# Column sums of two softmaxes taken in quarters on quarters of the array, and their inverses spread through DRAM

## The chip, the core and the metric

The kernel runs on one core of a Trainium2 chip. The metric is device time in microseconds (us) of one execution, lower is better. Five engines work side by side, each through its own queue: TensorE (PE in the profile, with its weight loads as PEld), VectorE (DVE), ScalarE (ACT), GpSimd (POOL) and SyncE (SP), which here only issues DMA transfers.

## What is computed

Four layers follow one another on `x`, eight samples of 512 channels by 1024 positions, float32. Layers 1 and 2 are the ones that matter here: each is an attention over the 1024 positions with a softmax, and the softmax needs one sum of exponentials for every position.

```python
# layer 1 (x: 8 samples, 512 channels, N = 1024 positions)
h = _group_norm(x, gamma, beta).reshape(B, C, N)
q, k, v = wq @ h + bq, wk @ h + bk, wv @ h + bv          # written as einsums
logits = jnp.einsum('bcn,bcm->bnm', q, k) * scale
attn = jax.nn.softmax(logits, axis=-1)                   # e / sum over m of e
o = jnp.einsum('bnm,bcm->bcn', attn, v)
x = x + wp @ o + bp
...
# layer 2 (t, p, g of 128 channels each)
s = jnp.einsum('ncq,nck->nqk', t, p)
s = jax.nn.softmax(s * SCALE, axis=2)                    # e / sum over k of e
att = jnp.einsum('nqv,ncv->ncq', s, g)
z = Z_w @ att                                            # then an affine map, and + x
```

Layer 0 is an attention without a softmax, divided by the largest singular value of its map; layer 3 multiplies signs of the activations by signs of weights and applies a piecewise linear function.

## The kernel before

A first stage of some 230 us loads all inputs, makes layer 0's maps and folds layer 1's four weight matrices into two. Then the function `fast` runs once for each of the eight samples, in some 210 us each: layer 1, layer 2 and layer 3 of that sample, with the beginning of the next sample's work woven in. Everything is float32 on TensorE but for layer 3's signs. Products of layer 1 are done with seven block products in place of eight (`seven`, `product_of`, `values1`).

The exponentials are kept transposed: a tile `e` holds 128 of the summed-over positions on its partitions and all 1024 output positions along its rows. A softmax's denominator is therefore a sum over partitions and over eight tiles `e`. VectorE adds the eight tiles into one tile `esum` of 128 x 1024, and TensorE adds over the partitions, with a matrix of ones as weights. That last step, the inverse, and the spreading of the inverse over all 128 partitions is the function `inverse_sums` (lines 822 to 844), which the change rewrites. Before the change it does this:

- Two matmuls (line 826), one for each half of the positions (`half(h)`, 512 columns). The weights are 64 columns of ones, so each matmul writes 64 equal rows: half 0 to partitions 0 to 63 of one PSUM bank (`side(0)`), half 1 to partitions 64 to 127. A float32 matmul is two instructions in the trace, so these are four.
- One VectorE reciprocal of the whole bank, 128 x 512 (line 834), into the tile `rsum`.
- Four DMAs (line 838), each of 64 partitions by 2 KB: each half of `rsum` is copied to both halves of the partitions of `rfull`, which is 128 x 2 x 512. After that each partition holds all 1024 inverses.
- Two DMAs of 2 KB (line 840) that copy the inverses to four rows of `guard`, a table that is checked once at the end of the kernel (`count_bad`); if a value in it is out of bounds, a slower general version is run.

`inverse_sums` is called at two places, 15 times in all. For layer 1 it is called in all eight samples, in the middle of the product `make_v` (line 916); the inverse is first used in `values1` (line 593), after the rest of `make_v` and the first eight groups of `values1`' products. For layer 2 it is called in the first seven samples (line 969); the eighth uses `inverse_rows`, which has no DMA on its path and is not changed.

The layer 2 call is the tight one. TensorE's order around it is written out in `fast`, and the trace has it in that order: two eighths of the product for half 0 (`values2(0, range(0, 2))`), then `inverse_sums`, then the other six eighths for half 0 and four eighths for half 1 (lines 970 to 972, matmuls at line 951), and then `close2` (line 674), which multiplies by `att`. `att` is that product times the inverses (line 960, on VectorE). So the inverse must go through the reciprocal, the DMA and the `att` multiply in the time of 10 products, or TensorE waits. After `close2` the rest of the sample follows, in `leave` (layer 3) and in `make_u` of the next sample.

Within an engine's queue instructions start in order, and waits are on semaphores. All DMAs named here are issued by SyncE, which has the loads of `x`, the stores of the output and the stores and loads of `f_dram` in the same queue. `f_dram` is a scratch array in DRAM: layer 0's map `f` is written to it (line 1365) and read back per sample (line 282).

Of the kernel before, what the change touches and what calls it, by code (L numbers as in the profile page):

```python
# [8 lines left out]
F32 = mybir.dt.float32  # L9
# [7 lines left out]
P = 128  # L17
B = 8
C = 512
N = 1024  # L20
CC = C // P
NT = N // P
HF = 512
NH = N // HF
NTH = HF // P
MID = 64
# [59 lines left out]
def kernel(  # L86
# [17 lines left out]
    nc = tc.nc  # L104
# [9 lines left out]
    dram = ctx.enter_context(tc.tile_pool(name="dram", bufs=1, space=bass.MemoryType.DRAM))  # L114
# [8 lines left out]
    def bank():  # L123
        return psum["bank"].tile([P, HF], F32, tag="bank", name="bank")
# [17 lines left out]
    def half(i):  # L142
        return bass.ts(i, HF)

    def side(i):

        return slice(i * MID, (i + 1) * MID)
# [93 lines left out]

    f_dram = [dram.tile([P, HF], F32, name=f"f_dram{b}") for b in range(B)]
    gm = [keep.tile([P, 3, P], F32, tag=f"gm{j}", name=f"gm{j}") for j in range(NPAIR)]
    sw3 = wpool.tile([P, CC, C // 2], F16, tag="sw3", name="sw3")
# [574 lines left out]

    def inverse_sums(env, esum, row):

        ps = bank()
        for h in range(NH):
            mm(  # L826
                out=ps[side(h), :],
                lhsT=ones2[:, 0:MID],
                rhs=esum[:, half(h)],
                start=True,  # L830
                stop=True,
            )
        r = env["small"].tile([P, HF], F32, tag="rsum", name="rsum", bufs=1)
        nc.vector.reciprocal(r, ps)  # L834
        full = env["small"].tile([P, NH, HF], F32, tag="rfull", name="rfull", bufs=1)
        for h in range(NH):
            for i in range(2):
                nc.sync.dma_start(out=full[side(i), h, :], in_=r[side(h), :])
        for h in range(NH):
            nc.sync.dma_start(  # L840
                out=guard[4 * row : 4 * row + 4, h, :],
                in_=r[h * MID : h * MID + 1, :].rearrange("o (a b) -> o a b", b=P),
            )
        return full

    def inverse_rows(env, esum, row):
# [31 lines left out]
    def fast(env, n, hb, ua):  # L878
# [35 lines left out]
        for k, _ in enumerate(make_v(hb, vt)):  # L914
            if k == 3:
                r = inverse_sums(env, esum, n)
            if k == 5:
                next(ahead, None)
            chore(2)
# [47 lines left out]
        values2(0, range(0, 2))  # L967
        if more:
            r = inverse_sums(env, esum, B + n)
            values2(0, range(2, NTH))  # L970
            att = values2(0, range(NTH, NT))
# [151 lines left out]
    env = {}  # L1123
# [252 lines left out]
    ps = bank()  # L1376
# [5 lines left out]
    ps = bank()  # L1382
# [83 lines left out]
    ones2 = late.tile([P, P], F32, tag="ones2", name="ones2")  # L1466
    nc.vector.memset(ones2, 1.0)
    guard = late.tile([2 * B * 4, NH, P], F32, tag="guard", name="guard")
# [3 lines left out]
    with ExitStack() as main:  # L1472
# [3 lines left out]
        small = main.enter_context(tc.tile_pool(name="small", bufs=3))  # L1476
# [122 lines left out]
    with tc.If(verdict[0] > 0):  # L1599
        with (  # L1600
# [5 lines left out]
            env = {"big": big, "e": epool, "small": small}  # L1606
# [49 lines left out]
```

## Time and profile before

| | us |
|---|---|
| median of three runs | 1911.45 (1911.01 to 1911.63) |
| the profiled execution, its own time | 1911.79 |
| its span, from the first instruction to the last | 1909.9 |
| TensorE busy in that span | 1886.4 |
| VectorE busy | 1130.2 |
| ScalarE busy | 510.3 |
| GpSimd busy | 224.5 |
| the 15 reciprocals of line 834 | 50.4 |

The profile shows one execution. A row of the timeline gives the start of a group of instructions, the time from the first one's start to the last one's end, the engine, the line, the operation with output and inputs, the shape, and how many; in brackets stands how long the engine was idle just before and what ended that. Matmuls are pipelined: one of 512 columns in float32 is listed with 592 ns, but in a row of them each starts about 0.43 us after the one before, so their listed lengths overlap.

### The profile page before, as it was taken

To read this page: it belongs to the slowest core of one execution; us is meant where nothing else is said; L and a number is where in the kernel's file an instruction comes from. 1 tells how busy PE (TensorE), PEld (TensorE's weight loads), DVE (VectorE), ACT (ScalarE), POOL (GpSimd) and SP (SyncE) were. 2 spreads that over 40 slices of the span, in tenths; PEclk is the share of its full clock that TensorE was granted. 3 is DMA by queue.
4 is the path that set the end of the run, shared out by engine and by line. 5 is a ranking of instruction groups with operands and counts; after the bars stand their busy time and mean duration, and the time that the engine had idled before them with its cause. 6 is when DMAs were issued, how large, how long until landed. Compare 5 with 4: busy or idle time off the path is not lost.

```text
span 1909.9 us, 16334 instructions
## 1 busy us (share of the span) xinstructions
PE 1886.4 (99%) x6118; PEld 977.5 (51%) x6118; DVE 1130.2 (59%) x1762; ACT 510.3 (27%) x811; POOL 224.5 (12%) x176
## 2 busy tenths in 40 slices
PE   9999999999999999999999999999999999999997
PEld 4366456544745447444645446544645455544653
DVE  3256676448664677447664676457753775466547
ACT  2142121134212332035202431034202521234014
POOL 0000011201121011200121011201120011101121
PEclk9999999999999999999999999999999999999999
DMA  8420000002000120002000120002000200010001
GB/s 320 159 78 6 0 6 12 1 12 88 17 1 0 34 72 12 1 11 88 17 1 0 38 68 12 0 13 87 11 1 9 91 12 0 1 34 22 12 0 46
DMA packets 27782, 66.45 MB, mean 35 GB/s; under 512 B 4272, under 2 KB 5424, under 8 KB 27056
## 3 DMA queue, kind: packets, MB, share of 16 engines
q1 hardware_dynamic: 26768, 64.90, 10.1%
q8 instruction: 50, 0.82, 0.2%
q10 hardware_dynamic: 864, 0.43, 0.1%
q14 instruction: 36, 0.29, 0.1%
q0 software_dynamic: 64, 0.00, 0.0%
HBM read 38.51 MB, written 18.87 MB: 30 GB/s over the span
## 4 chain that ended last, share of the span: by engine, by line
PE 92%; DVE 7%; issue 1%; ACT 1%; DMA 0%; POOL 0%; DVEq 0%; ACTq 0%
PE bank L387 42%; PE bank L556 20%; PE bank L951 6%; PE bank L805 6%; PE bank L1241 5%; PE bank L657 3%; PE bank L411 2%; PE bank L674 2%; DVE both L748 1%; DVE both L718 1%; PE wide L1281 1%; PE wide L1335 1%; PE bank L1022 1%; PE bank L1023 1%; PE bank L697 1%; PE bank L826 1%
## 5 line engine op out<-in xcount | busy, mean ns | idle before, releaser
L556 PE MATMUL bank<-e,vt 128*128 128x512 f32 x768 | 334.2, 593 | 0.0
L556 PEld LDWEIGHTS bank<-e,vt 128*128 128x128 f32 x768 | 144.9, 190 | 174.8 <-issue 173.2
L387 PE MATMUL bank<-ut,h 128*128 128x512 f32 x384 | 182.3, 597 | 0.0
L344 DVE TENSOR_TENSOR e<-bank,e 128x512 f32<-128x512 f32 x128 | 87.8, 686 | 81.9 <-PE bank L387 80.8
L387 PE MATMUL bank<-us,hs 128*128 128x512 f32 x256 | 121.5, 597 | 1.3 <-DVE us L316 0.5
L387 PEld LDWEIGHTS bank<-ut,h 128*128 128x128 f32 x384 | 71.4, 190 | 95.6 <-issue 84.0
L951 PE MATMUL bank<-e,tpg 128*128 128x512 f32 x256 | 114.7, 595 | 0.0
L805 PE MATMUL bank<-tpg 128*128 128x512 f32 x256 | 114.6, 592 | 0.0
L812 ACT ACTIVATE e<-bank 128x512 f32<-128x512 f32 x128 | 76.4, 597 | 128.6 <-PE bank L805 128.6
L387 PE MATMUL bank<-h,wu 128*128 128x512 f32 x192 | 90.4, 593 | 2.4 <-DVE h L462 1.7
L387 PE MATMUL bank<-wo,h 128*128 128x256 f32 x384 | 91.8, 382 | 0.0
L817 DVE TENSOR_TENSOR esum<-esum,e 128x1024 f32<-128x1024 f32 x48 | 58.8, 1225 | 54.9 <-ACT e L812 54.9
L359 POOL TENSOR_TENSOR e<-e 128x512 f32<-128x512 f32 x32 | 43.4, 1356 | 403.8 <-ACT e L338 238.3
L951 PEld LDWEIGHTS bank<-e,tpg 128*128 128x128 f32 x256 | 48.1, 190 | 63.2 <-issue 63.1
L805 PEld LDWEIGHTS bank<-tpg 128*128 128x128 f32 x256 | 48.6, 190 | 60.7 <-issue 60.5
L387 PEld LDWEIGHTS bank<-wo,h 128*128 128x128 f32 x384 | 71.6, 190 | 13.5 <-ACT vt L338 4.1
L359 POOL TENSOR_TENSOR ut<-ut 128x512 f32<-128x512 f32 x16 | 21.7, 1359 | 476.1 <-ACT ut L340 476.1
L344 DVE TENSOR_TENSOR vt<-bank,vt 128x512 f32<-128x512 f32 x64 | 44.1, 689 | 56.2 <-PE bank L387 55.8
L387 PEld LDWEIGHTS bank<-us,hs 128*128 128x128 f32 x256 | 47.1, 190 | 54.9 <-issue 48.3
L834 DVE RECIPROCAL rsum<-bank 128x512 f32<-128x512 f32 x15 | 50.4, 3358 | 38.2 <-PE bank L826 38.2
L685 ACT ACTIVATE sg<-xt,rb 128x512 f16<-128x512 f32 x64 | 45.0, 718 | 103.7 <-DVE xt L676 100.2
L1241 PE MATMUL bank<-xt,fg 128*64 128x512 f32 x256 | 59.5, 613 | 4.6 <-DMA fg<-in_w_fg 4.6
(330 smaller groups left out, 3017.2 us busy)
## 6 DMA issues: line engine op xcount, KB each, us to landing
xt<-in_x SPq DMA_DIRECT2D x55, 512.0 KB
out<-both SPq DMA_DIRECT2D x63, 256.0 KB
rfull<-rsum SPq DMA_DIRECT2D x60, 128.0 KB
f_dram<-f SPq DMA_DIRECT2D x8, 256.0 KB
fb<-f_dram SPq DMA_DIRECT2D x8, 256.0 KB
w<-in_w SPq DMA_DIRECT2D x1, 1024.0 KB
q<-in_w_q SPq DMA_DIRECT2D x1, 1024.0 KB
k<-in_w_k SPq DMA_DIRECT2D x1, 1024.0 KB
```

What stands on the lines that cost most here:

```text
L344: nc.vector.tensor_tensor(dst, ps, u, ALU.add)
L359: nc.gpsimd.tensor_tensor(c22, c22, c12, ALU.add)
L387: mm(out=ps[:, q * w : (q + 1) * w], lhsT=lt(ka, kb, q, k), rhs=rhs(ka, kb, q, k), start=first and q == 0 and k == 0, stop=last and k == 1 ...
L556: mm(out=ps, lhsT=a[:, t, bass.ts(r_, P)], rhs=e[t], start=first and t == 0, stop=last and t == NTH - 1, skip_group_check=True,)
L657: mm(out=ps[:, i, :], lhsT=xt[:, cc, bass.ts(4 * h + i, P)], rhs=sbw["tpg"][:, cc, 2 * P : 3 * P], start=cc == 0, stop=cc == CC - 1,)
L685: nc.scalar.activation(sg[:, cc, :], xt[:, cc, half(h)], AF.Sign, bias=rb3[:, cc : cc + 1])
L805: mm(out=ps, lhsT=pt[:, 0, bass.ts(t, P)], rhs=tt[:, 0, half(h)], start=True, stop=True,)
L812: nc.scalar.activation(e[:, half(h)], ps, AF.Exp, scale=float(P) ** -0.5)
L817: nc.vector.tensor_tensor(esum, esum, e, ALU.add)
L834: nc.vector.reciprocal(r, ps)
L951: mm(out=banks[h], lhsT=gt[:, t, :], rhs=es[t][:, half(h)], start=t == 0, stop=t == NT - 1,)
L1241: mm(out=banks[i][side(h), :], lhsT=w0[i][:, cc, :], rhs=xt[:, cc, half(h)], start=cc == 0, stop=cc == CC - 1,)
```

## The change

`inverse_sums` works on quarters of the positions. Four matmuls take the place of two: each has 32 columns of ones as weights and 256 positions, and writes 32 equal rows to its own quarter of the partitions, at its own quarter of the array's columns (`tile_position`). The reciprocal is then of 128 x 256. One row of each quarter (partitions 0, 32, 64 and 96, 1 KB each) is written by one DMA to a new scratch array in DRAM, `r_dram[row]`, of 4 KB; one DMA reads these 4 KB 128 times, once for each partition of `rfull` (512 KB in all), and one more reads them into the four rows of `guard`. There are 16 arrays `r_dram`, one for each row number, so none is used twice. Both reads need the write to have landed, and all three are issued by SyncE.

```diff
+    r_dram = [dram.tile([4, N // 4], F32, name=f"r_dram{i}") for i in range(2 * B)]
     f_dram = [dram.tile([P, HF], F32, name=f"f_dram{b}") for b in range(B)]
...
     def inverse_sums(env, esum, row):
 
+
+        g, w = 4, N // 4
         ps = bank()
-        for h in range(NH):
+        for q in range(g):
             mm(
-                out=ps[side(h), :],
-                lhsT=ones2[:, 0:MID],
-                rhs=esum[:, half(h)],
+                out=ps[bass.ts(q, P // g), 0:w],
+                lhsT=ones2[:, 0 : P // g],
+                rhs=esum[:, bass.ts(q, w)],
                 start=True,
                 stop=True,
+                tile_position=(0, q * P // g),
             )
-        r = env["small"].tile([P, HF], F32, tag="rsum", name="rsum", bufs=1)
-        nc.vector.reciprocal(r, ps)
+        r = env["small"].tile([P, w], F32, tag="rsum", name="rsum", bufs=1)
+        nc.vector.reciprocal(r, ps[:, 0:w])
+        nc.sync.dma_start(
+            out=r_dram[row], in_=r.rearrange("(q i) n -> q i n", q=g)[:, 0, :]
+        )
         full = env["small"].tile([P, NH, HF], F32, tag="rfull", name="rfull", bufs=1)
-        for h in range(NH):
-            for i in range(2):
-                nc.sync.dma_start(out=full[side(i), h, :], in_=r[side(h), :])
-        for h in range(NH):
-            nc.sync.dma_start(
-                out=guard[4 * row : 4 * row + 4, h, :],
-                in_=r[h * MID : h * MID + 1, :].rearrange("o (a b) -> o a b", b=P),
-            )
+        nc.sync.dma_start(
+            out=full.rearrange("p h n -> p (h n)"),
+            in_=r_dram[row].rearrange("q n -> (q n)").partition_broadcast(P),
+        )
+        nc.sync.dma_start(
+            out=guard[4 * row : 4 * row + 4, :, :],
+            in_=r_dram[row].rearrange("(h j) (a b) -> (j a) h b", h=NH, b=P),
+        )
         return full
```

## The prediction

> **What bounds the kernel now.** I read the shares of the page first, then a table of stages, then the timeline around one call of the changed function.
>
> ```profile
> PE 1886.4 (99%) x6118; PEld 977.5 (51%) x6118; DVE 1130.2 (59%) x1762; ACT 510.3 (27%) x811; POOL 224.5 (12%) x176
> ```
>
> Busy shares of engines in three stretches (us, then busy and count for PE, PEld, DVE, ACT, POOL, then clock, DMA share, GB/s):
>
> ```profile
> 230.00:1890.00 1660.00, 1659.19 (x5044) 857.30 (x5043) 1009.32 (x1469) 445.73 (x701) 205.50 (x142) 1.00 0.07 23
> 1890.00:1910.00 20.00, 9.77 (x36) 3.79 (x34) 13.47 (x21) 10.04 (x16) 7.87 (x6) 0.85 0.30 109
> 0.00:230.00 230.00, 217.40 (x1042) 116.39 (x1043) 107.44 (x273) 54.54 (x96) 11.11 (x28) 1.00 0.32 117
> ```
>
> From 230 to 1890 us, which holds all 15 calls, TensorE is idle for 0.8 us in 1660. Two rules follow there: TensorE time that is taken away shortens the run, and any wait that the change puts on TensorE lengthens it. VectorE time is worth something only through a wait of TensorE.
>
> Timeline of TensorE at the first call for layer 2:
>
> ```profile
> 402.32 1.88 PE L951 MATMUL bank<-e,tpg 128*128 128x512 f32 x4
> 404.13 1.08 PE L826 MATMUL bank<-esum,ones 128*64 128x512 f32 x4
> 405.14 8.85 PE L951 MATMUL bank<-e,tpg 128*128 128x512 f32 x20
> 413.83 3.60 PE L674 MATMUL bank<-att,z 128*128 128x512 f32 x8
> ```
>
> The same call on VectorE and on SyncE's DMA queue:
>
> ```profile
> 405.26 3.36 DVE L834 RECIPROCAL rsum<-bank 128x512 f32<-128x512 f32 x1 [3.65 <-PE bank L826]
> 408.64 2.44 SPq L838 DMA_DIRECT2D rfull<-rsum  x4
> 411.13 1.30 SPq L840 DMA_DIRECT2D guard<-rsum  x2
> 411.70 0.69 DVE L960 TENSOR_TENSOR att<-bank,rfull 128x512 f32<-128x512 f32 x1 [3.09 <-DMA rfull<-rsum]
> ```
>
> The reader is to see two things. First, the four matmul instructions of line 826 take 1.08 us, not four times 0.43: the two halves of the array's columns run at the same time, so there are two rounds. Second, `att` ends at 411.70 + 0.69 = 412.39, and its user, line 674, starts at 413.83 directly behind the matmuls before it: 1.4 us to spare (1.0 us if its first weight load, at 413.40, is what must wait). The other six calls for layer 2 look the same within 0.1 us where I looked at them (626, 844, 1060 and 1681 us). For layer 1 the inverse is made at 287 us and first used at 315.8 us (line 593).
>
> **What the Trainium skill says.** "TensorEngine Tiling (Array Packing)", Available Configurations and Key Properties: with all 128 rows in use the array can be split in two tiles of 64 columns or four of 32; tiles run at the same time; a change of the mode drains the engine. The trace agrees for two tiles (the rounds above) and shows the drain; no run here shows four. "TensorE: Matmul & The Clock Gate", Measured speedup vs the span model: three column tiles of 32 gave 2.38 times, by a model of one matmul plus about 4 ns for each further tile. "DMA: Bandwidth & Descriptors", Rules for kernel authors: a DMA that reads what another wrote must wait for the first one's completion semaphore. The trace agrees: the first read of `f_dram` waited 1.4 us for its write. The same page, How many engines: a transfer over 4 partitions is spread over 4 of the 16 DMA engines. No run here shows that, and for 4 KB it is small.
>
> **The matmuls.** What a call costs TensorE now: the L951 row of four starts at 402.32, so in an unbroken row the next instruction would start at 402.32 + 4 x 0.428 = 404.03. (0.428 comes from the row of eight of line 674: 3.60 = 7 steps + 0.592.) The next L951 row starts at 405.14 and is 8.85 long where 19 x 0.428 + 0.592 = 8.72 would do. A call thus takes 405.14 - 404.03 + 0.13 = 1.24 us: two rounds of 0.428, and 0.38 around them for the changes of mode. After the change there are eight instructions of 256 columns. The 128x256 matmuls of line 387 in `make_v` step by (1.89 - 0.38) / 7 = 0.216 us. If four run at once, that is two rounds of 0.216, and with some 0.02 us for starting four one after another and the same 0.38 around them, 0.83 us. Gain 0.41 us per call, times 15 = 6.1 us. Bounds: 0 if only two of the four run at once (four rounds of 0.216), less than 0 only if they ran one by one, which the two-tile rounds speak against; at the top 0.45 us if the drain of a shorter matmul is shorter too, 6.8 us. I take 0.41. Weight loads double to eight; the four now are done within 0.20 us beside the matmuls, so I cost them at nothing.
>
> **The reciprocal.** 3.36 us for 512 columns, 0.16 us for the reciprocals of one column (line 1077), so for 256 about 0.16 + 3.20 / 2 = 1.76 us. VectorE gets 15 x 1.6 = 24 us back. Nothing waits for it but the inverse itself: for layer 2 VectorE is idle for 3.09 us just after it, and for layer 1 the use is 28 us away. Worth nothing on the path, except as time for the transfers.
>
> **The transfers.** They gain a wait: the read waits on SyncE for the write to land. Behind it in that queue stand only the guard's read and then, at 430 us, the stores of the output, so the queue itself blocks nobody. Worked out for the call at 404 us, with times of the trace before:
>
> - last matmul ends 0.41 us earlier, at 404.80; reciprocal from 404.85 to 406.61.
> - The write, 4 KB, issued at 406.63. Nearest row, `f_dram`:
>
> ```profile
> 106.48 1.02 SPq L1365 DMA_DIRECT2D f_dram<-f  x2
> 108.95 0.32 SPq L282 DMA_DIRECT2D fb<-f_dram  x1
> ```
>
> The read went out 2.47 us after the write's issue, for 256 KB and with another load under way: the upper bound. In the row of rfull above, the first bytes moved 1.1 us after the issue, by the DMA view, and `att` began about 0.5 us after the bytes of its half had moved: 1.6 us is the lower bound. I take 1.8: the read goes out at 408.45.
> - The read, 512 KB: 1.0 us to the first byte as above, 1.5 us at the 350 GB/s that loads of `x` reach, 0.5 us to land: 3.0 us, so 411.45. At the 200 GB/s at which the four copies move now it is 2.6 us of bytes, and 412.55.
> - `att` takes 0.69 us: done at 412.15. It is wanted at 413.83 - 0.41 = 413.42, or at 412.99 by the weight load.
>
> That leaves 0.8 to 1.3 us. The transfer chain is one link longer, and the halved reciprocal and the single issue in place of four (2.44 us of issuing) pay for it. With both upper bounds (write + 0.7, read + 1.1) `att` ends at 413.95 and TensorE waits 0.5 to 1.0 us, seven times: 3.7 to 6.7 us. For layer 1 any of this is hidden by 28 us of matmuls. The guard's read is wanted at the end of the kernel and costs nothing.
>
> **Sum.** 1911.79 of the profiled execution, less 6.1, is 1905.7; it stands 0.34 above the median, so 1905.35 against the median of 1911.45. A measurement of this kernel tells 0.2%, 3.8 us, from no change.
>
> **Rivals.**
>
> - *The broadcast is slow, and TensorE waits for it* (the slower side). One mechanism: 16 DMA engines read the same 4 KB of DRAM at the same time, and `att` waits for the whole 512 KB, where now it waits for the half that it uses. It decides from 411.45 + 0.85 on, that is, once the read takes over 3.9 us; it undoes the whole gain at 0.87 us more, and the run is slower by 0.2% from 1.4 us more. At 130 GB/s the bytes take 4.0 us, 2.5 more than taken; 1.65 us of wait, times 7, is 11.5 us: 1911.45 - 6.1 + 11.5 = 1916.9. For it: nothing in the trace reads the same few KB 128 times undisturbed. Against it: `bg_row`, 128 reads of the same 512 bytes, passes in the first 50 us without a gap in the DMA view. Chance 0.13.
> - *Four tiles run no better than two.* The time on TensorE is unchanged: 1911.4. For it: only two at once are seen here. Chance 0.13.
> - *A part of the gain is lost in short waits* (write and read near their upper bounds, half of the seven margins used up, 2.5 to 5 us): 1909. Chance 0.10.
> - *The order of instructions shifts.* Another length of the transfers could make the framework put some matmuls in another order, in `leave`, where VectorE is 16.04 of 17 us busy (423 to 440). That could cost or bring 3 us; 1902.5 to 1908.5 around the forecast, half of it outside. Chance 0.07.
> - *As forecast*, own range 1904.3 to 1907.4: chance 0.57.
>
> **Chances.** Faster by over 0.2%: 0.57, with a part of the short waits and most of the shifted order, 0.68. Within 0.2%: 0.18. Slower: 0.14. The range reaches from 1903.8, a gain of 6.8 with a little from the order, to 1911.6, which takes in the two cases without gain and leaves out the slow broadcast.
>
> **What would show it.** Line 826: eight instructions in about 0.65 us in place of 1.08. The reciprocal near 1.76 us. A write issued within 0.05 us of its end, the read 1.6 to 2.5 us after the write, `att` starting near 411.45 on this clock and line 674 directly behind line 951, with no wait for `att`. Wrong if line 826 keeps its 1.08 us, or if line 674 shows a wait that ends with `att`, seven times.

## The result, and the profile after

The changed kernel takes 1904.61 us, the median of 7 runs (1904.21 to 1906.04), beside 1910.65 us for seven runs of the kernel before (1910.15 to 1911.63). The ratio is 0.9969, with a 95% interval of 0.996 to 0.9979: 6.0 us faster, where 6.1 were forecast. (The forecast of 1905.35 us started from a median of 1911.45; the kernel before is 0.8 us lower in these runs.) The profiled execution took 1906.04 us, with a span of 1904.3. The lines named before move down: line 826 is now 829, 834 is 838, 951 is 958, 960 is 967 and 674 is 675.

Busy time of the engines on the page of after (us, share of the span, instructions):

```profile
PE 1880.0 (99%) x6178; PEld 976.9 (51%) x6178; DVE 1106.2 (58%) x1762; ACT 510.2 (27%) x811; POOL 224.3 (12%) x176
```

The stretch with all 15 calls, in the table of stages of after (us, then busy and count for PE, PEld, DVE, ACT, POOL, then clock, DMA share, GB/s):

```profile
230.00:1884.00 1654.00, 1653.19 (x5104) 857.25 (x5103) 985.61 (x1470) 446.05 (x701) 205.34 (x142) 1.00 0.06 23
```

TensorE is idle for 0.8 us in this stretch, as it was before, and with 60 instructions more (four at each of 15 calls) its busy time is some 6 us less. So the time did not come out of a wait: TensorE needs less time for the same sums. The ends of that stretch are whole microseconds; two matmuls that both kernels have bound it more sharply. One is the first product of `so` and `hs`, 6 us ahead of the first call, the other the first matmul of `close2` in the eighth sample, behind the last call. Before:

```profile
276.82 1.89 PE L387 MATMUL bank<-so,hs 128*128 128x256 f32 x8
1880.97 3.60 PE L674 MATMUL bank<-att,z 128*128 128x512 f32 x8
```

After:

```profile
277.05 1.89 PE L388 MATMUL bank<-so,hs 128*128 128x256 f32 x8
1874.60 3.60 PE L675 MATMUL bank<-att,z 128*128 128x512 f32 x8
```

That is 1604.15 us before and 1597.55 after: 6.60 us less, 0.44 for each of 15 calls. VectorE's busy time in the stretch of the table fell by 1009.32 - 985.61 = 23.7 us, nearly four times as much, and that bought nothing by itself.

TensorE in the timeline of after, at the first call for layer 2:

```profile
402.10 1.88 PE L958 MATMUL bank<-e,tpg 128*128 128x512 f32 x4
403.91 0.64 PE L829 MATMUL bank<-esum,ones 128*32 128x256 f32 x8
404.48 8.85 PE L958 MATMUL bank<-e,tpg 128*128 128x512 f32 x20
413.17 3.60 PE L675 MATMUL bank<-att,z 128*128 128x512 f32 x8
```

The same call on VectorE and on SyncE's DMA queue:

```profile
404.62 1.76 DVE L838 RECIPROCAL rsum<-bank 128x256 f32<-128x256 f32 x1 [3.23 <-PE bank L829]
406.41 0.53 SPq L839 DMA_DIRECT2D r_dram<-rsum  x1
408.05 0.35 SPq L843 DMA_DIRECT2D rfull<-r_dram  x1
408.45 0.32 SPq L847 DMA_DIRECT2D guard<-r_dram  x1
411.84 0.69 DVE L967 TENSOR_TENSOR att<-bank,rfull 128x512 f32<-128x512 f32 x1 [5.46 <-DMA rfull<-r_dram]
```

And the first weight load of line 675, in the timeline of PEld:

```profile
412.74 0.19 PEld L675 LDWEIGHTS bank<-att,z 128*128 128x128 f32 x1 [0.24 <-DVE att L967]
```

The reader is to see three things. The eight matmul instructions of line 829 take 0.64 us where four took 1.08. The chain behind them (reciprocal, write, read, `att`) is one link longer than before: VectorE is idle for 5.46 us ahead of `att`, where it was 3.09. And TensorE does not notice: `att` ends at 412.53, and line 675 starts at 413.17, directly behind line 958 (404.48 + 8.85 - 0.592 + 0.428 = 413.17). In the list of TensorE's waits in after no entry names `att`; the bracket of the weight load above does, but the 0.24 us in it are the idle time that every weight load of such a row has before it.

The broadcast in the DMA view of after, from 406 to 412.5 us in 40 slices of 0.1625 us (the first row is the busy share of the DMA engines in tenths):

```profile
DMA  0000000000000000004499989990632100000000
GB/s 0 0 0 0 0 0 0 0 0 19 6 0 0 0 0 0 0 0 151 151 353 403 403 328 403 353 151 6 214 158 101 50 25 0 0 0 0 0 0 0
```

The write is the small hump at 407.5 us. The 512 KB of the read begin at 409.0 us, 1.0 us after its issue, and run at 330 to 400 GB/s. The slice at 410.4 us looks like a gap and is none: the view counts a packet whole where it starts, and the 14 packets of 4 KB that start between 410.17 and 410.31 take 0.37 us each in the mean, where most take 0.16. A tail with fewer and fewer packets follows, until 411.4; `att` begins 0.5 us after that.

### The profile page after: what moved, and what is told of

It is laid out like the page before. It is cut to its first block, busy times and chain, and to the rows that moved or that the text cites. A ratio compares the mean times of both kernels' runs of the same rounds, so it can differ in the third digit from the quotient of the medians.

```text
span 1904.3 us, 16364 instructions
## 1 busy us (share of the span) xinstructions
PE 1880.0 (99%) x6178; PEld 976.9 (51%) x6178; DVE 1106.2 (58%) x1762; ACT 510.2 (27%) x811; POOL 224.3 (12%) x176
## 4 chain that ended last, share of the span: by engine, by line
PE 92%; DVE 7%; issue 1%; ACT 1%; DMA 0%; POOL 0%; DVEq 0%; ACTq 0%
PE bank L388 42%; PE bank L557 20%; PE bank L958 6%; PE bank L806 6%; PE bank L1248 5%; PE bank L658 3%; PE bank L412 2%; PE bank L675 2%; DVE both L749 1%; DVE both L719 1%; PE wide L1288 1%; PE wide L1342 1%; PE bank L1029 1%; PE bank L1030 1%; PE bank L698 1%; DVE xt L677 1%
## 5 line engine op out<-in xcount | busy, mean ns | idle before, releaser
L658 PEld LDWEIGHTS bank<-tpg,xt 128*128 128x128 f32 x512 | 59.5, 192 | 7.2 <-issue 7.2
```

The costliest lines, as they stand in the source:

```text
L658: mm(out=ps[:, i, :], lhsT=xt[:, cc, bass.ts(4 * h + i, P)], rhs=sbw["tpg"][:, cc, 2 * P : 3 * P], start=cc == 0, stop=cc == CC - 1,)
```

## The experiments

The rivals to test: that the gain is TensorE's time in the sums (the forecast); that it is VectorE's shorter reciprocal, or the smaller number of DMAs; and that the way through DRAM costs something on its own. Runs of the kernel before on the same chips had a median of 1911.1 us (44 runs, beside the way through DRAM, each layer alone, and most of the sum on VectorE) and 1911.19 us (17 runs, beside the other four).

### The way through DRAM alone

```diff
-        for q in range(g):
+        for h in range(NH):
             mm(
-                out=ps[bass.ts(q, P // g), 0:w],
-                lhsT=ones2[:, 0 : P // g],
-                rhs=esum[:, bass.ts(q, w)],
+                out=ps[side(h), :],
+                lhsT=ones2[:, 0:MID],
+                rhs=esum[:, half(h)],
...
-        nc.vector.reciprocal(r, ps[:, 0:w])
+        nc.vector.reciprocal(r, ps)
         nc.sync.dma_start(
-            out=r_dram[row], in_=r.rearrange("(q i) n -> q i n", q=g)[:, 0, :]
+            out=r_dram[row].rearrange("(h j) n -> h (j n)", h=NH),
+            in_=r.rearrange("(h i) n -> h i n", h=NH)[:, 0, :],
```

The sums by halves and the long reciprocal of before, the transfers of after.

> Two halves on two column tiles and a reciprocal of 128x512 as before, but spread through DRAM as in the change. Theory A (the gain is TensorE time of the sums, and the shorter reciprocal pays for the longer way through DRAM): line 829's matmuls take 1.08 us again, so no gain; the reciprocal ends at 408.62 on the clock of before, the way through DRAM takes the 5.44 us measured after the change, att ends at 414.75 where line 675 wants it at 413.83: about 0.95 us of wait on TensorE, seven times, so about 6.7 us more than before, 1917. Rival B (the gain is VectorE's shorter reciprocal): 1910.7, as before. Rival C (the gain is in the fewer DMAs): 1904.6, as after.

Measured: 1911.57 us (1910.83 to 1912.9), ratio 1.0003 (0.9995 to 1.0012). TensorE in the timeline of this kernel, with the weight loads and the rest left out:

```profile
404.14 1.08 PE L827 MATMUL bank<-esum,ones 128*64 128x512 f32 x4
405.15 10.57 PE L956 MATMUL bank<-e,tpg 128*128 128x512 f32 x24
415.55 3.60 PE L675 MATMUL bank<-att,z 128*128 128x512 f32 x8
```

The expected wait did not come, and the line of 24 says why. The framework put twelve products (24 instructions) between the sums and `close2`, where before and after have ten, so `att` had 1.72 us more of cover; it ends 1.0 us early here, and 0.75 to 1.13 us early over the seven calls:

```profile
413.89 0.69 DVE L965 TENSOR_TENSOR att<-bank,rfull 128x512 f32<-128x512 f32 x1 [5.27 <-DMA rfull<-r_dram]
```

What follows: replacing six DMAs by three gains nothing, so that theory falls. Nor does the other order gain or lose anything: the stretch between the two matmuls named above takes 1604.15 us, as before. Matmuls and reciprocal are both the old ones here, so those two are not told apart; and the wait was not tested. That took another run.

### The same with TensorE's order held

The order in which the matmuls are queued is kept as before by order-only edges: everything after the first `close2` is issued behind its last matmul.

```diff
-            close2(xt, att, 0)
-            att = values2(1, range(NTH, NT))
-            fill()
-            for _ in leave(env, xt, dst, [0]):
+            with tc.issue_after(close2(xt, att, 0).ins):
+                att = values2(1, range(NTH, NT))
+                fill()
+                for _ in leave(env, xt, dst, [0]):
...
```

> As the run with halves through DRAM, but TensorE's order after the call is tied to that of before (close2 straight after ten products), so no later products can be put ahead of it. Theory A: att ends 413.89 + 0.69 = 414.58 on that run's clock, line 675 would start at 413.83: 0.8 us of wait, seven times, 5.5 us: 1916.6, and the wait is seen on line 675. Rival (what is lost there is made up in layer 3, which is VectorE's): under 1912.5.

Measured: 1918.51 us (1917.15 to 1918.93), ratio 1.0037 (1.0024 to 1.0049), so 4.6 to 9.4 us slower than before. From the list of TensorE's waits of this kernel (us in total, times, longest):

```profile
PE bank L675 <- DVE att L966: 4.9, 7, 0.9
```

And its timeline of TensorE and VectorE:

```profile
404.20 8.85 PE L957 MATMUL bank<-e,tpg 128*128 128x512 f32 x20
...
412.81 0.69 DVE L966 TENSOR_TENSOR att<-bank,rfull 128x512 f32<-128x512 f32 x1 [5.14 <-DMA rfull<-r_dram]
...
413.56 3.70 PE L675 MATMUL bank<-att,z 128*128 128x512 f32 x8 [0.51 <-DVE att L966]
```

In an unbroken row line 675 would start at 404.20 + 8.85 - 0.592 + 0.428 = 412.89. It starts 0.67 us later, 0.06 us after `att` ends at 413.50, and its row is 0.10 us longer: 0.77 us in this call. Over the seven calls line 675 starts 0.58 to 1.10 us late, 6.0 us in all, and each row is 0.10 us longer: 6.7 us. By exactly that the stretch between the two matmuls has grown (1610.86 us), and the order of TensorE's instructions is that of before throughout, so the order-only edges cost nothing beside the waits. The slower rival's mechanism is real: once the chain overruns the products queued in front of `close2`, TensorE waits in every layer 2 call. What keeps the changed kernel, which has this order around `close2`, on the good side is the halved reciprocal: 1.60 us of time in the chain, more than any of the seven waits.

### Each layer alone

The old function is kept beside the new one under the name `inverse_halves`, and one of the two calls uses it. For layer 1 alone:

```diff
-            r = inverse_sums(env, esum, B + n)
+            r = inverse_halves(env, esum, B + n)
```

> The change in layer 1's eight calls alone, layer 2's seven as before. Theory A: 8 x 0.41 = 3.3 us less than before, 1907.4. Rival (only layer 2's calls gain, since the inverse is on the path there alone): 1910.7.

For layer 2 alone:

```diff
-                r = inverse_sums(env, esum, n)
+                r = inverse_halves(env, esum, n)
```

> The change in layer 2's seven calls alone, layer 1's eight as before. Theory A: 7 x 0.41 = 2.9 us less than before, 1907.8; with the run of layer 1 alone it adds up to the whole 6. Rival (the longer transfers give back a part in layer 2): less than 2 us gained here, and over 3.5 in layer 1.

Measured: layer 1 alone 1907.32 us (1906.74 to 1908.08), ratio 0.9981 (0.9973 to 0.9989); layer 2 alone 1908.34 us (1907.17 to 1909.31), ratio 0.9985 (0.9979 to 0.9992). That is 3.8 and 2.8 us by the medians, where 0.41 us for each of eight and seven calls had made 3.3 and 2.9 the forecast. The two parts add up to the whole within what the measurement tells. The stretch between the two matmuls tells them apart more finely: 3.52 and 3.07 us less than before, 0.44 for each of the eight and each of the seven calls. Layer 1's calls have 28 us of cover and so no chain to speak of, and they gain as much per call as the tight ones: the gain is in the matmuls, and the tight calls lose none of it to their chain.

### The matmuls twice

```diff
-        for q in range(g):
+        for q in list(range(g)) * 2:
```

Every quarter's sum is made twice, into the same place.

> The changed kernel with the four quarter matmuls issued twice (the second time writes the same sums again). Theory A (four tiles run at once, and the rest of a call's cost is the change of mode): the eight added instructions cost 2 x 0.216 = 0.43 us a call, 15 x 0.43 = 6.5 us more than the changed kernel: 1911.1. Rival (only two tiles at once and a cheaper change of mode): 0.86 us a call, 13 us, 1917.5.

Measured: 1911.7 us (1910.54 to 1912.11), ratio 1.0004 (0.9995 to 1.0013), which is (1.0004 - 0.9969) x 1911 = 6.7 us above after. In its timeline of TensorE:

```profile
402.71 1.07 PE L829 MATMUL bank<-esum,ones 128*32 128x256 f32 x16
403.71 8.85 PE L958 MATMUL bank<-e,tpg 128*128 128x512 f32 x20
```

Eight more instructions lengthen the group by 1.07 - 0.64 = 0.43 us, two rounds of 0.216. So four tiles run at once also when they follow one another. Of the 0.77 us that a call of after costs (from the table at the end of the experiments), 0.43 belong to the matmuls, and the other 0.34 are paid once per call, whatever its number of rounds.

### The guard's read first

```diff
-        nc.sync.dma_start(
-            out=full.rearrange("p h n -> p (h n)"),
-            in_=r_dram[row].rearrange("q n -> (q n)").partition_broadcast(P),
-        )
         nc.sync.dma_start(
             out=guard[4 * row : 4 * row + 4, :, :],
             in_=r_dram[row].rearrange("(h j) (a b) -> (j a) h b", h=NH, b=P),
         )
+        nc.sync.dma_start(
+            out=full.rearrange("p h n -> p (h n)"),
+            in_=r_dram[row].rearrange("q n -> (q n)").partition_broadcast(P),
+        )
```

Asked whether the tail of the broadcast comes from the guard's small pieces, which are issued 0.4 us behind it.

> The guard's read is issued ahead of the broadcast. Theory A: the broadcast goes out 0.4 us later, att begins at most 0.4 us later than the 3.8 us after the broadcast's issue, and the time stays within 0.2% of 1904.6, since about 0.6 us were left. Rival (the guard's small read, behind the broadcast, is what holds its last packets up): the broadcast lands in under 3.4 us from its issue.

Measured once: 1905.37 us. On SyncE's queue and on VectorE in its timeline:

```profile
407.55 0.27 SPq L843 DMA_DIRECT2D guard<-r_dram  x1
407.91 0.33 SPq L847 DMA_DIRECT2D rfull<-r_dram  x1
...
411.65 0.69 DVE L967 TENSOR_TENSOR att<-bank,rfull 128x512 f32<-128x512 f32 x1 [5.78 <-DMA rfull<-r_dram]
```

From the broadcast's issue to `att` it is 3.74 us, as against 3.79 in after, with the guard's pieces ahead of it; over the seven calls 3.48 to 4.13, as against 3.72 to 4.18. So it is not the guard's pieces behind it that hold up its last packets. What makes the tail stays open. (Eleven products stand ahead of `close2` in this kernel, so its margins are not those of after.)

### Most of the sum on VectorE

VectorE transposes `esum` in blocks of 32 x 32 and adds along the rows, which leaves 128 x 32; one matmul with `fold32` (a matrix of ones and zeros that adds the four groups of partitions) makes all sums.

```diff
+        nc.vector.transpose(full.rearrange("p h n -> p (h n)"), esum)
+        part = small.tile([P, w], F32, tag="part", name="part", bufs=1)
+        nc.vector.tensor_reduce(
+            part, full.rearrange("p h (b j) -> p (h b) j", j=32), AX.X, ALU.add
+        )
...
+        mm(out=ps[:, 0:w], lhsT=fold32, rhs=part, start=True, stop=True)
+        r = small.tile([P, 2, w], F32, tag="rsum", name="rsum", bufs=1)
+        nc.vector.reciprocal(r[:, 0, :], ps[:, 0:w])
+        nc.vector.transpose(r[0:32, 1, :], r[0:32, 0, :])
         nc.sync.dma_start(
-            out=r_dram[row], in_=r.rearrange("(q i) n -> q i n", q=g)[:, 0, :]
+            out=r_dram[row].rearrange("q (i n) -> (q i) n", n=w), in_=r[0:32, 1, :]
```

> VectorE does most of the sum over partitions (transpose of 32x32 blocks and a sum over 32), TensorE only adds four groups with one matmul of 128 weights and 32 columns, without a change of the array's mode. Theory A: a call costs TensorE 0.12 us in place of 0.83 us, 15 x 0.71 = 10.7 us less than after: 1894, and VectorE's busy time goes up by some 15 us without a cost. Rival B (VectorE's time is what counts): not under 1904.6, rather 1906 to 1912.

Measured: 1899.02 us (1897.79 to 1899.43), ratio 0.9936 (0.9923 to 0.995). Busy time on its page:

```profile
PE 1872.9 (99%) x6088; PEld 976.8 (51%) x6088; DVE 1128.2 (59%) x1809; ACT 510.0 (27%) x811; POOL 225.4 (12%) x176
```

Its timeline of TensorE at the same call:

```profile
401.38 1.88 PE L956 MATMUL bank<-e,tpg 128*128 128x512 f32 x4
403.12 0.41 PE L834 MATMUL bank<-part,fold 128*128 128x32 f32 x2
403.37 8.83 PE L956 MATMUL bank<-e,tpg 128*128 128x512 f32 x20
```

VectorE is busy for 22 us more than in after (1128.2 against 1106.2), nearly all that the change had freed, and the run is another 5.6 us faster (6.8 in the stretch between the two matmuls). So VectorE's time is not what the change gained. The fall of TensorE's busy time, 1880.0 - 1872.9 = 7.1 us, carries it again. It was less than forecast, because the small matmul costs more than the 0.12 us taken for it: the next product could start at 401.38 + 4 x 0.43 = 403.10 without it, it starts at 403.37, and its row is 0.07 us longer than 19 x 0.43 + 0.59 = 8.76, which makes some 0.35 us. (The 0.39 us that the next expectation takes over comes from the prediction's step of 0.428, which is a little short.) The operand is late there: `part` is ready only at 403.07, after the weight load's usual time at 402.67, and the load comes at 403.12 together with the matmul. At the first call of layer 1 the two instructions start in their turn, at 282.91, and the next matmul follows 0.16 us later. Over the 15 calls it is 0.31 us a call (from the same table). How much of that is the lateness and how much the two weight loads that nothing covers was not separated.

### No matmul in the sums

As above, but the four groups' sums go through DRAM, too: they are written to `p_dram`, read back on 32 partitions side by side, and added, inverted and written on from there. Against the kernel with blocks:

```diff
-        mm(out=ps[:, 0:w], lhsT=fold32, rhs=part, start=True, stop=True)
+        nc.vector.transpose(part[:, 1, :], part[:, 0, :])
+        nc.sync.dma_start(out=p_dram[row], in_=part[:, 1, :])
+        four = small.tile([32, 4, w], F32, tag="four", name="four", bufs=1)
+        nc.sync.dma_start(out=four, in_=p_dram[row].rearrange("(a b) i -> b a i", a=4))
+        r = small.tile([32, w], F32, tag="rsum", name="rsum", bufs=1)
+        nc.vector.tensor_reduce(r, four.rearrange("b a i -> b i a"), AX.X, ALU.add)
+        nc.vector.reciprocal(r, r)
...
```

> No matmul for these sums at all: VectorE sums blocks of 32 partitions, the four groups go to DRAM, come back on 32 partitions, are added and inverted there, go to DRAM again and are broadcast. Theory A: the 0.39 us that the block version still spends on TensorE per call goes, 15 x 0.39 = 5.9 us: 1893; the two more trips (about 3.5 us) are covered because the framework puts all sixteen products ahead of close2. Rival (the longer way puts att, and with it layer 3's work on VectorE, so late that TensorE waits there): 1899 or more.

Measured: 1892.62 us (1892.28 to 1893.64), ratio 0.9905 (0.9889 to 0.9922), the fastest version here. Busy time on its page:

```profile
PE 1867.0 (99%) x6058; PEld 974.9 (52%) x6058; DVE 1132.1 (60%) x1822; ACT 510.0 (27%) x811; POOL 225.8 (12%) x176
```

Its timeline of TensorE, and the four links on SyncE and VectorE:

```profile
399.61 13.90 PE L957 MATMUL bank<-e,tpg 128*128 128x512 f32 x32
...
401.57 0.35 SPq L835 DMA_DIRECT2D p_dram<-part  x1
...
403.01 0.30 SPq L837 DMA_DIRECT2D four<-p_dram  x1
...
406.80 0.34 SPq L842 DMA_DIRECT2D rfull<-r_dram  x1
...
410.57 0.69 DVE L966 TENSOR_TENSOR att<-bank,rfull 128x512 f32<-128x512 f32 x1 [5.20 <-DMA rfull<-r_dram]
...
413.34 3.60 PE L676 MATMUL bank<-att,z 128*128 128x512 f32 x8
```

Two ways through DRAM follow one another, and `att` still ends 2.1 us early (411.26 to 413.34; 1.2 to 2.5 us over the seven calls), because all sixteen products of line 957 now stand in one row ahead of `close2`. From after it gains 12.0 us by the medians. With the sums off TensorE nothing of them is left in the time.

All traces can be compared between the two matmuls named with the result. In each kernel the same 4808 matmul instructions lie between them, besides those of the sums:

| kernel | from | to | us between | against before |
|---|---|---|---|---|
| before | 276.82 | 1880.97 | 1604.15 | |
| after | 277.05 | 1874.60 | 1597.55 | -6.60 |
| the way through DRAM alone | 276.83 | 1880.98 | 1604.15 | 0.00 |
| the same, order held | 275.89 | 1886.75 | 1610.86 | +6.71 |
| layer 1 alone | 276.18 | 1876.81 | 1600.63 | -3.52 |
| layer 2 alone | 276.85 | 1877.93 | 1601.08 | -3.07 |
| the matmuls twice | 275.41 | 1879.41 | 1604.00 | -0.15 |
| the guard's read first | 276.54 | 1874.07 | 1597.53 | -6.62 |
| most of the sum on VectorE | 276.85 | 1867.58 | 1590.73 | -13.42 |
| no matmul in the sums | 275.32 | 1861.35 | 1586.03 | -18.12 |

The last kernel has no sums on TensorE and no wait for `att`, so what the others have over it, divided by 15, is what a call costs: 1.21 us before, 0.77 after, 1.20 with the matmuls twice, 0.31 with blocks. What lies outside this stretch varies by more than a microsecond from one execution to the next (the starts by 1.7 us), which is a part of the noise in the medians.

## Why the prediction was right, and where it was off

- **What bounds the kernel.** Right. TensorE's idle time in the stretch with the calls stayed at 0.8 us, and the gain is its lost time in the sums, 15 x 0.44 us. The last two kernels give VectorE more work than after does and are faster.
- **The matmuls, 0.41 us a call.** Right. Counted as in the prediction, the next product of after starts at 404.48 where 402.10 + 4 x 0.428 = 403.81 would do, and its row is 0.13 longer: 0.80 us a call, where 0.83 was forecast and 1.24 reckoned before. There is a slip in that count: 3.60 - 0.592 over seven steps is 0.430, not 0.428, so both calls come out too high by some 0.03 us; the table has 1.21 and 0.77. The difference, 0.44 us, is hardly touched. The page on array tiling, "TensorEngine Tiling (Array Packing)", Key Properties, in the Trainium skill says that different tiles can work in parallel; for four tiles of 32 columns the 0.64 us of line 829 now agrees, and the doubled matmuls confirm it. That refutes the rival in which four run no better than two. The time around the rounds was taken over unchanged from the two-tile call, and it hardly changed: 1.21 - 2 x 0.43 = 0.35 us before, 0.77 - 2 x 0.216 = 0.34 after. That it is all for the changes of mode, as the prediction has it, is not shown: the kernel with blocks makes its sums on the whole array and still pays 0.31 us for a matmul of 32 columns.
- **The reciprocal, 1.76 us.** Right, and right that it is worth nothing but time for the transfers. There it decides: with the old one and the old order the run is slower than before. With the old one and an order that puts two more products ahead of `close2` it is as fast as before.
- **The write, 1.8 us from its issue to the read's.** It is 1.64, near the lower bound that was worked out.
- **The read, 3.0 us to `att`.** This term was mis-sized: 3.79 us in this call, and 3.72 to 4.18 over the seven, close to the 3.9 from which the slower rival was to decide. By its parts, from the packets of the call shown: 0.98 us to the first byte (1.0 taken), 2.36 us until the last byte had moved (1.5 taken), 0.45 us more until `att` began (0.5 taken). So the bytes were mis-sized. The 350 GB/s hold in the body (330 to 400), but with the tail the whole 512 KB come to 220 GB/s, near the 200 from which the prediction made its upper bound. An estimate from the Trainium skill, "DMA: Bandwidth & Descriptors", Anatomy of one DMA, 2.0 us plus the bytes at 436 GB/s, gives 3.2 us for 512 KB, also short of the measured 3.79; that fit is for DMAs issued by GpSimd, and these are SyncE's.
- **The margin, 0.8 to 1.3 us.** It came out at 0.64 us to the matmul and 0.21 us to its weight load in the call shown. Over the seven calls it is 0.60 to 0.71 us to the matmul in six, and 0.28 us in the last. The error in the read is all of it: 0.79 more there, 0.16 less in the write. The tail cost no time because the margin was wide enough, not because the read was rightly sized. In the last call the bytes were through as early as in the others (3.39 us after the issue, as against 3.30 to 3.41), but `att` began 0.8 us after them and not 0.4; why stays open. That call also shows which deadline counts:

```profile
1684.06 0.69 DVE L967 TENSOR_TENSOR att<-bank,rfull 128x512 f32<-128x512 f32 x1 [5.83 <-DMA rfull<-r_dram]
1684.81 0.41 PEld L675 LDWEIGHTS bank<-att,z 128*128 128x128 f32 x2 [0.44 <-DVE att L967]
1685.03 3.60 PE L675 MATMUL bank<-att,z 128*128 128x512 f32 x8
```

The weight load is held up until `att` has ended, 0.21 us beyond its usual time, and the matmul still starts in its turn with a row of the usual length. So the matmul's start is the deadline, not the weight load 0.43 us before. In the held order, where `att` missed both, the matmul began 0.06 us after `att` and its row was 0.10 us longer.
- **The rivals.** The slow broadcast did not decide, by those 0.28 to 0.7 us. It was nearer than its chance of 0.13 made it look. The shifted order did not show in after: the order of instructions on TensorE is that of before but for one swap, in layer 1. It did show in four of the experiments, each with another chain: twelve products ahead of `close2` in the way through DRAM alone, eleven with the guard's read first, all sixteen without matmuls, and swaps in layer 1 with blocks.

## What to carry to other kernels

Where TensorE is busy for 99% of a stretch, price a change by TensorE's time alone, round by round, with an excursion to narrower tiles in a dense stream of wide matmuls charged once on top (here 0.34 us a call, nearly half of it); then ask whether the sum needs TensorE at all. A longer chain on the other engines is free as long as it fits under the products queued ahead of its user, so work out that margin for every call, the last one too, and count a margin as open when it is smaller than the uncertainty of one transfer. When an experiment takes a chain apart, compare the order of instructions before the times. And where the medians lie within the noise, compare the traces between two instructions that all kernels have.

## What was not expected of the hardware

- A DRAM array of 4 KB read 128 times at once moved its bytes at 330 to 400 GB/s in the body, as fast as loads of large arrays do, but the last fifth of its packets took 0.7 to 1.0 us in each of the 15 reads of after, which the guard's read behind it doesn't explain.
- Two short float32 matmul instructions of 32 columns, with full 128 x 128 weights, held up a dense row of products by some 0.35 us in the call shown, nearly as long as one instruction of 512 columns (0.43).
- A second pass through DRAM, 1.44 us from the write's issue to the read's (401.57 to 403.01) and 1.63 more until VectorE began to use it (404.64), cost TensorE nothing here; the matmul that it replaced cost 0.31 us a call.
